# A two-layer image kernel: inverse roots on GpSimd, the LayerNorm variance with positions on partitions, and a new order within the scan's step

## The chip, the cores and the metric

The kernel runs on one core of a Trainium2 chip, as one launch. The metric is the device time of that launch in microseconds (us). Before the change the median of three runs is 4572.44 us (4570.81 to 4586.5). Five engines take part, each with its own queue of instructions: TensorE (PE in the profile, with its weight loads as PEld), VectorE (DVE), ScalarE (ACT), GpSimd (POOL) and SyncE (SP), which here only starts DMAs.

## The reference

The input is `x` of shape (4, 48, 48, 128). Two layers are computed, each as `x = x + layer(groupnorm(x))`. The change touches the first layer nearly alone:

```python
def _L0_conv_ref(x, ...):                       # d = 256, N = 16 states, K = 4 directions, R = 8
    xin, z = split(x @ in_proj_w.T)             # 256 + 256 channels
    xc = silu(depthwise_conv_3x3(xin) + conv_b)
    xs = stack([rows, columns, rows reversed, columns reversed])    # 4 directions of 2304 positions
    dts_r, Bs, Cs = split(x_proj(xs))
    dt = softplus(dt_proj(dts_r) + dt_proj_b)
    A  = -exp(A_logs)
    h  = h * exp(dt * A) + (dt * u) * B         # a scan over the positions, for 256 channels x 16 states
    y  = sum_n(h * C) + Ds * xs                 # the four directions are summed
    y  = (y - mean(y)) * rsqrt(var(y) + 1e-05) * norm_g + norm_b    # over the 256 channels
    return (y * silu(z)) @ out_proj_w.T

def _gn(v, G=32, eps=1e-5):                     # ahead of both layers
    return (v - mean) / sqrt(var + eps)         # mean and var over a group of 4 channels
```

The second layer (Fourier operators and an attention over 32 heads) gets only its group norm's root changed.

## The kernel before

**Layout.** In the first layer the channels lie on the partitions, as two halves `f` of 128, and the positions along the free axis. An image has 2304 positions in five chunks of 480, 480, 480, 480 and 384. The order of the work is image by image, four directions each in the order `ORDER` (0, 2, 1, 3), five chunks each (backwards for directions 2 and 3), and 16 states each: 4 x 4 x 5 x 16 = 1280 steps. The layer takes the span from about 60 to 3779 us; the second layer follows it.

**The step.** `advance` (L807) puts a new step into a window of nine and runs the list `LAGS` (L800-804): each stage works on the step that lies so many places back, so the work of one step is spread over nine turns of the loop. Every instruction of the first layer is recorded by one helper (class `Ordered`, all of them line L55 in the profile), which keeps each engine in program order. So the place of a stage in `LAGS` is its place in the queues. The stages are:

- `fetch` loads the row of C for the step into `cbc`, on SP's queue, spread over the partitions by the DMA. `cbc` has four buffers.
- An even state is "plain": PE transposes a column of B into `pb` (`spread`), DVE multiplies `db = du * pb` (`drive_in`), POOL writes the two columns between the halves from the carry (`open_db`), and ACT's Exp writes the decay into PSUM, tile `da` (`decay_here`).
- An odd state is "turned": ACT scales a transposed `du` by B (`scaled`, stage `scale`), PE transposes that back into PSUM `da` (`turn`), and ACT's Exp writes `decay` into SBUF (`decay_there`).
- `scan`: one DVE instruction, `h = decay * h + db` along the positions, for both halves. Its two forms in the profile are `h<-da,carry,db` (plain) and `h<-decay,carry,da` (turned).
- `carry_on` copies the last column of `h` for the next chunk, and `read_out` multiplies `hc = h * cbc`, both on POOL.
- `sum_plain` and `sum_turned`: PE transposes `hc` and adds it up over the states in PSUM `yp`. After state 15 `put_away` has ACT copy `yp` to the tile `turned`, and sends it to memory or starts `gather`.

**The side work.** All else is written as generators that stand in the list `later`: `end_piece` and `begin_piece` (two entries of `LAGS`) run one of them by one piece each step. `begin_piece` runs a generator up to its next PE work, and `end_piece` runs what follows on the other engines. The generators that matter here are: `front` (L249: group norm, `widen`, and ten `convolve`s of the next image), `project` and `project_chunk` (dt, B and C of a chunk for the next direction), `turn_du` (the transposed `du`), `gather` (the two directions of a chunk brought together), `back` (L460: LayerNorm, gate and output projection of one chunk, five for each image, 20 in all) and `matrices` (L263: during the last image it builds what the second layer needs, from many small DMAs on SP's queue). `front` or `matrices` starts when no `back` of the image before is left. After `begin()` all side work shares one PSUM bank, tag `pp`.

**ACT's tables.** ACT holds the tables of a set of functions; where the next function is not in the set, the program has an `ACT_TABLE_LOAD`. The step needs Exp, and the gates need Tanh, which stand with no load between them. `clump` (L445) runs Softplus over the dt of a whole direction. It is called at state 4 of the last chunk (L892-894), ahead of the step. `back` takes the inverse root of the variance as `exp(-0.5 * ln(v + eps))`: Ln at one yield and Exp in place two pieces later, both on 128 x n values, since `lnmat` (a 128 x 128 matrix of 1/256) puts the variance on every partition. `group_affine` (L911), called once for each image and twice in the second layer, takes Sqrt on ACT and a reciprocal on DVE.

**Idle transposes.** `warm` (L781) has PE transpose the identity three times into the bank `pp`, on every second step, if no side work is held on PE. Nothing reads the result.

The planner has no costs and no due times; the order of the queues is the order in which the generators and stages run.

Of the kernel before, what the change touches and what calls it, by code (L numbers as in the profile page):

```python
# [10 lines left out]
F32 = mybir.dt.float32  # L11
BF16 = mybir.dt.bfloat16
AF = mybir.ActivationFunctionType
ALU = mybir.AluOpType
# [44 lines left out]
def first_layer(ctx, tc, io, x1_dram, sp_dram, d_w, d_m):  # L59
# [79 lines left out]
        on.vector.tensor_scalar(w_out[:, 0, f], w_out[:, 0, f], ln_g[:, f : f + 1], None, ALU.mult)  # L139
    eps = const.tile([128, 1], F32, name="eps")  # L140
    on.gpsimd.memset(eps, 1e-5)
    ddiag = const.tile([128, NF, 128], F32, name="ddiag")
    for f in range(NF):
        on.vector.tensor_scalar(ddiag[:, f], ident, ds_sum[:, f : f + 1], None, ALU.mult)
# [26 lines left out]
    def open_up(b, x, made):  # L171

        xc = two.tile([128, NF, L], F32, tag="xc", name=f"xc{b}")
        made["xc"] = xc
        st = small.tile([128, 6, 6], F32, tag="st", name=f"st{b}", bufs=1)
        for q in range(6):
            on.vector.bn_stats(st[:, q], x[:, 0, q * 384 : (q + 1) * 384])
            if q % 2:
                yield FREE
        mv = small.tile([128, 2], F32, tag="mv", name=f"mv{b}")  # L180
        on.vector.bn_aggr(mv, st)
        aff = small.tile([128, 2], F32, tag="aff", name=f"aff{b}")
        group_affine(on, small, ps_s, gmat, eps, mv[:, 0:1], mv[:, 1:2], aff[:, 0:1], aff[:, 1:2], 1, f"g{b}")
        yield FREE
        wb = small.tile([128, NF], F32, tag="wb", name=f"wb{b}")
        pw = side(f"pw{b}")
        for f in range(NF):
            on.tensor.matmul(
                pw[:, f : f + 1], w_z[:, f * 128 : (f + 1) * 128], aff[:, 1:2], start=True, stop=True
            )  # L190
        on.scalar.activation(wb, pw[:, 0:NF], AF.Copy, scale=0.5)
        w = two.tile([128, D], F32, tag="w", name=f"w{b}")
        on.gpsimd.tensor_scalar(w, w_z, aff[:, 0:1], None, ALU.mult)
        made["w"], made["wb"], made["aff"] = w, wb, aff
        yield FREE

    def widen(b, x, aff, engine):

# [11 lines left out]
    def convolve(b, f, pad, xc, s, n):  # L210
        ends = (1, 3, 5, 7, 8) if b < 2 else (1, 2, 3, 4, 5, 6, 8)
        r0, nr = s // H, n // H
        pc = side(f"pc{b}_{f}_{s}")
        for j in range(9):
            dy, dx = divmod(j, 3)
            on.tensor.matmul(
                pc[:, 0:n].rearrange("p (r c) -> p r c", c=H),
                w_c[:, j, f * 128 : (f + 1) * 128],
                pad[:, r0 + dy : r0 + dy + nr, dx : dx + H],
                start=(j == 0),  # L220
                stop=(j == 8),
            )
            if j in ends:
                yield None if j == 8 else MORE
        v = xc[:, f, s : s + n]
        th = one.tile([128, LC], F32, tag="th", name=f"th{b}_{f}_{s}")[:, 0:n]
        on.scalar.activation(v, pc[:, 0:n], AF.Identity, bias=cb[:, f : f + 1], scale=0.5)
        on.scalar.activation(th, pc[:, 0:n], AF.Tanh, bias=cb[:, f : f + 1], scale=0.5)
        on.vector.scalar_tensor_tensor(v, th, 1.0, v, ALU.add, ALU.mult)

    def boot(chunks, made):

# [144 lines left out]
    def project_chunk(c, w_dt, xc):  # L377


        k, s, n = c.k, c.s, c.n  # L380
        if k < 2:
            src = at(xc, k, s, n)
            px = side(f"px{c.t}")
            for f in range(NF):
                on.tensor.matmul(
                    like(px[0 : PAIR + NX, 0:n], k), w_xp[:, k, f], src[:, f], start=(f == 0), stop=(f == NF - 1)
                )
                yield MORE if f == 0 else None
# [41 lines left out]
    def project(b, k, chunks, xc):  # L430
# [11 lines left out]
        projected.append(chunks)  # L442
        yield FREE

    def clump():  # L445

        while projected:
# [12 lines left out]
    def back(b, s, n, yb, x, w, wb):  # L460
# [9 lines left out]
        xp = one.tile([128, LC], F32, tag="th", name=f"xp{t}")[:, 0:n]  # L470
        on.gpsimd.tensor_copy(like(xp, 1), xs)
        pm = side(f"pm{t}")
        for f in range(NF):
# [4 lines left out]
        on.scalar.activation(z[:, :, 0:n], ys, AF.Square)  # L478
        yield FREE
        pv = side(f"pv{t}")  # L480
        for f in range(NF):
            on.tensor.matmul(pv[:, 0:n], lnmat, z[:, f, 0:n], start=(f == 0), stop=(f == NF - 1))
        yield

        on.scalar.activation(rs[:, 0:n], pv[:, 0:n], AF.Ln, bias=eps)
        yield FREE
        for f in range(NF):
            pz = side(f"pz{t}_{f}")
# [300 lines left out]
    step_i = [0]  # L789

    def drain(gen):
        if gen in later:
            later.remove(gen)
# [4 lines left out]

    decay_here, decay_there = partial(decay, turned=False), partial(decay, turned=True)
    LAGS = (  # L800
        (8, sum_plain), (3, fetch), (2, open_db), (4, drive_in), (5, scan), (3, spread), (7, sum_turned),
        (3, decay_there), (6, carry_on), (4, turn), (2, scale), (4, decay_here), (None, end_piece), (8, put_away),
        (None, begin_piece), (None, warm), (5, read_out),
    )
    window = deque([None] * 9, 9)

    def advance(u):  # L807
        window.appendleft(u)
        step_i[0] += 1
        for lag, stage in LAGS:  # L810
            if lag is None:
                stage()
# [42 lines left out]
    for j, chunks in enumerate(directions):  # L855
# [8 lines left out]
        for m, c in enumerate(chunks):  # L864
            c.carry = carries[j % 2]
            c.next = chunks[m + 1] if m + 1 < len(chunks) else directions[j + 1][0] if k < 2 else None
            for i in range(N):
# [66 lines left out]
def layer1(ctx, tc, io, x1_dram, out):  # L934
# [38 lines left out]
    fw = load("fw", [128, 66], io["c_FW"])  # L973
    eps = const.tile([128, 1], F32, name="eps1")
    nc.gpsimd.memset(eps, 1e-5)
    mean_m = const.tile([128, 32], F32, name="mean_m")
    nc.gpsimd.memset(mean_m, 1.0 / (H * W))
    over_h = const.tile([H, H], F32, name="over_h")
# [21 lines left out]
    def statistics(psum, p, x):  # L1000
# [8 lines left out]
        group_affine(on, small, psum, gmat, eps, mv[:, :, 0], mv[:, :, 1], aff[:, 0], aff[:, 1], 2, f"l1{p}")  # L1009
        return aff  # L1010

    def forward_w(psum, work, p, x, aff):
# [1173 lines left out]
```

## Time and profile before

| | us |
|---|---|
| median of three runs | 4572.44 |
| the profiled run | 4572.95 |
| its span | 4571.2 |
| around the span | 1.75 |
| first layer, boot (to about 60) | 60 |
| first layer, 1280 steps | about 60 to 3745 |
| last `back` and change of layers | 3745 to 3803 |
| second layer | 3803 to 4571 |

The page's table of the costliest groups gives the size of the parts. A line has: source line, engine, operation, the tile written and those read, the shapes, the count, then the busy time and the mean duration of one in ns, and the idle time just before them with what ended most of it. "(+1 forms)" says that chunks of 384 are averaged in.

```profile
L55 POOL TENSOR_TENSOR hc<-h,cbc 128x960 f32<-128x960 f32 (+1 forms) x1280 | 2544.1, 1990 | 618.7 <-PE yp L55 228.0
L55 DVE TENSOR_TENSOR_SCAN h<-da,carry,db 128x962 f32<-128x962 f32 (+1 forms) x640 | 1356.5, 2120 | 145.7 <-ACT da L55 136.8
L55 DVE TENSOR_TENSOR_SCAN h<-decay,carry,da 128x962 f32<-128x962 f32 (+1 forms) x640 | 1363.3, 2130 | 12.7 <-PE da L55 6.4
L55 DVE TENSOR_TENSOR db<-du,pb 128x960 f32<-128x960 f32 (+1 forms) x640 | 700.4, 1094 | 99.6 <-PE pb L55 88.0
```

DVE is thus busy for 3854.3 of 4571.2 us (84%), PE for 85%, ACT for 77%, POOL for 73%.

### The profile page before, as it was taken

To read this page: it belongs to the slowest core of one execution; us is meant where nothing else is said; L and a number is where in the kernel's file an instruction comes from. 1 tells how busy PE (TensorE), PEld (TensorE's weight loads), DVE (VectorE), ACT (ScalarE), POOL (GpSimd) and SP (SyncE) were. 2 spreads that over 40 slices of the span, in tenths; PEclk is the share of its full clock that TensorE was granted. 3 is DMA by queue.
4 is the path that set the end of the run, shared out by engine and by line. 5 is a ranking of instruction groups with operands and counts; after the bars stand their busy time and mean duration, and the time that the engine had idled before them with its cause. 6 is when DMAs were issued, how large, how long until landed. Compare 5 with 4: busy or idle time off the path is not lost. (4 is left out here: it accounts for less than half of the span.)

```text
span 4571.2 us, 74429 instructions
## 1 busy us (share of the span) xinstructions
PE 3878.1 (85%) x26572; PEld 3020.8 (66%) x26572; DVE 3854.3 (84%) x2646; ACT 3510.6 (77%) x7002; POOL 3335.4 (73%) x3494
## 2 busy tenths in 40 slices
PE   6989988888999878889998788878887875979877
PEld 3777777776777767767777677667777752545543
DVE  3988899989999999999989999979999974656446
ACT  3888888998888889988888899879999862323344
POOL 2777788878887888878878888768888861456432
PEclk8989999999999999999999999989999997989877
DMA  2334333333343343334333333334433332155536
GB/s 62 90 90 109 93 97 100 109 95 106 101 106 95 97 106 104 97 101 109 102 93 103 106 104 94 104 87 113 104 103 106 99 111 58 26 130 136 129 101 159
DMA packets 327070, 461.08 MB, mean 101 GB/s; under 512 B 112788, under 2 KB 295636, under 8 KB 325996
## 3 DMA queue, kind: packets, MB, share of 16 engines
q1 hardware_dynamic: 311904, 433.20, 36.0%
q10 hardware_dynamic: 14796, 23.13, 1.5%
q8 instruction: 210, 3.44, 0.3%
q14 instruction: 160, 1.31, 0.1%
HBM read 400.99 MB, written 55.44 MB: 100 GB/s over the span
## 5 line engine op out<-in xcount | busy, mean ns | idle before, releaser
L55 POOL TENSOR_TENSOR hc<-h,cbc 128x960 f32<-128x960 f32 (+1 forms) x1280 | 2544.1, 1990 | 618.7 <-PE yp L55 228.0
L55 DVE TENSOR_TENSOR_SCAN h<-da,carry,db 128x962 f32<-128x962 f32 (+1 forms) x640 | 1356.5, 2120 | 145.7 <-ACT da L55 136.8
L55 DVE TENSOR_TENSOR_SCAN h<-decay,carry,da 128x962 f32<-128x962 f32 (+1 forms) x640 | 1363.3, 2130 | 12.7 <-PE da L55 6.4
L55 PE MATMUL yp<-ident,hc 128*128 128x128 f32 (+1 forms) x9728 | 1221.5, 278 | 48.1 <-POOL hc L55 47.4
L55 PEld LDWEIGHTS yp<-ident,hc 128*128 128x128 f32 (+1 forms) x9728 | 1110.6, 141 | 198.0 <-issue 111.2
L55 ACT ACTIVATE scaled<-turned,bt 128x256 f32<-128x256 f32 (+1 forms) x2432 | 1034.4, 497 | 2.8 <-PE da L55 2.7
L55 ACT ACTIVATE da<-dt,a_neg 128x480 f32<-128x480 f32 (+1 forms) x1280 | 826.4, 646 | 191.2 <-DVE h L55 167.9
L55 ACT ACTIVATE decay<-dt,a_neg 128x480 f32<-128x480 f32 (+1 forms) x1280 | 800.1, 675 | 58.1 <-DVE h L55 34.0
L55 PE MATMUL da<-ident,scaled 128*128 128x128 f32 (+1 forms) x4864 | 640.1, 274 | 191.8 <-DVE h L55 174.2
L55 DVE TENSOR_TENSOR db<-du,pb 128x960 f32<-128x960 f32 (+1 forms) x640 | 700.4, 1094 | 99.6 <-PE pb L55 88.0
L55 PEld LDWEIGHTS da<-ident,scaled 128*128 128x128 f32 (+1 forms) x4864 | 537.3, 144 | 238.3 <-DVE h L55 103.3
L55 PEld LDWEIGHTS pb<-ident,bt 128*128 128x128 f32 (+1 forms) x2432 | 290.6, 140 | 178.5 <-issue 110.0
L55 PE MATMUL pb<-ident,bt 128*128 128x128 f32 (+1 forms) x2432 | 373.0, 275 | 34.9 <-DVE db L55 34.3
L55 PE MATMUL pc<-pad,w_c 128*128 128x480 f32 (+1 forms) x720 | 335.1, 579 | 13.3 <-ACT th L55 8.0
L55 POOL TENSOR_TENSOR du<-dt,xc 128x480 f32<-128x480 f32 (+1 forms) x160 | 205.9, 1287 | 49.3 <-ACT dt L55 49.3
L1599 POOL TENSOR_TENSOR v<-grep,xrep 128x768 f32<-128x768 f32 x96 | 174.9, 1823 | 90.5 <-PE acc L1603 48.8
L1603 PE MATMUL acc<-v,attn_c 128*64 128x384 f32 x1152 | 211.7, 505 | 28.9 <-DVE v L1595 15.7
L1595 DVE TENSOR_TENSOR v<-gp,xrep 128x1536 f32<-128x1536 f32 x96 | 167.9, 1756 | 77.5 <-PE acc L1603 44.7
L55 PEld LDWEIGHTS da<-carry,ident 128*128 128x128 f32 x1280 | 200.0, 197 | 0.0
L55 PE MATMUL da<-carry,ident 128*128 128x2 f32 x1280 | 196.7, 223 | 0.0
L55 POOL COPY carry<-h 128x2 f32<-128x2 f32 x1024 | 195.7, 191 | 0.0
L1603 PEld LDWEIGHTS acc<-v,attn_c 128*64 128x64 f32 x1152 | 120.2, 140 | 109.2 <-issue 51.9
(378 smaller groups left out, 4208.0 us busy)
## 6 DMA issues: line engine op xcount, KB each, us to landing
cbc<-cd SPq DMA_DIRECT2D x512, 240.0 KB
cbc<-other SPq DMA_DIRECT2D x512, 240.0 KB
xrep<-dxt SPq DMA_DIRECT2D x48, 576.0 KB
cbc<-cd SPq DMA_DIRECT2D x128, 192.0 KB
cbc<-other SPq DMA_DIRECT2D x128, 192.0 KB
yt<-turned ACTq DMA_DIRECT2D x40, 384.0 KB
old<-yt SPq DMA_DIRECT2D x40, 384.0 KB
grep<-dgt SPq DMA_DIRECT2D x16, 576.0 KB
```

Source lines behind the costliest of these rows:

```text
L55: return lambda *args, **kw: self._tc.keep_in_program_order(emit(*args, **kw))
L1595: nc.vector.tensor_mul(v, gp[:, None, :, 0:NC].to_broadcast([128, 2, 2, NC]), x[:, :, 0:2])
L1599: nc.gpsimd.tensor_mul(v3, r[:, 2:3].to_broadcast([128, 2, NC]), x[:, :, 2])
L1603: nc.tensor.matmul(acc[c][64 * b : 64 * b + 64, 0:NC], attn_c[:, 2 * pair + b, g, q], v[:, b, c] if c < 2 else v3[:, b], start=first, stop ...
```

## The change

The change has seven parts, all in the order of the diff:

- `back`: the variance is taken with the positions on the partitions, by one-column matmuls (`pv`, one column for each block of 128 positions), copied to `var` with eps added on ACT (Identity), raised to -0.5 on POOL (`ALU.pow` on 128 x 4), transposed back onto all partitions by PE (`pe`) and copied to `rs` by ACT. Ln and Exp go. There is one more pair of yields.
- `group_affine`: DVE adds 1e-5, POOL raises to -0.5, for Sqrt and reciprocal. It applies in both layers.
- `convolve`: the gate's last product is held back; `flush`, a new entry of `LAGS`, issues it in the next step, ahead of the scan. `project_chunk` flushes all first.
- `soften`: the softplus at state 4 of the last chunk is issued by an entry of `LAGS` within the step.
- `warm` is gone.
- `LAGS` has a new order; `fetch` goes from lag 3 to 2, `drive_in` from 4 to 3, and `put_away` from 8 to 7.
- In the first direction a further piece of side work runs in every third step, for every fifth.

```diff
+    half = const.tile([128, 1], F32, name="half")
+    on.gpsimd.memset(half, -0.5)
+    var = const.tile([LB, 4], F32, name="var")
+    on.gpsimd.memset(var, 1.0)
...
+    held_back = deque()
+
+    def later_on(work):
+        held_back.append([1, work])
+
+    def flush(every=False):
+        for item in list(held_back):
+            item[0] -= 1
+            if every or item[0] <= 0:
+                held_back.remove(item)
+                item[1]()
...
         on.scalar.activation(th, pc[:, 0:n], AF.Tanh, bias=cb[:, f : f + 1], scale=0.5)
-        on.vector.scalar_tensor_tensor(v, th, 1.0, v, ALU.add, ALU.mult)
+        later_on(lambda: on.vector.scalar_tensor_tensor(v, th, 1.0, v, ALU.add, ALU.mult))
...
         if k < 2:
+            flush(True)
             src = at(xc, k, s, n)
...
+    def soften():
+        if wanted[0]:
+            wanted[0] = False
+            clump()
...
         pv = side(f"pv{t}")
-        for f in range(NF):
-            on.tensor.matmul(pv[:, 0:n], lnmat, z[:, f, 0:n], start=(f == 0), stop=(f == NF - 1))
+        for q, r in blocks(n):
+            for f in range(NF):
+                on.tensor.matmul(
+                    pv[0:r, q : q + 1],
+                    z[:, f, q * LB : q * LB + r],
+                    lnmat[:, 0:1],
+                    start=(f == 0),
+                    stop=(f == NF - 1),
+                )
         yield
-        on.scalar.activation(rs[:, 0:n], pv[:, 0:n], AF.Ln, bias=eps)
+        for q, m, r in runs(n):
+            on.scalar.activation(var[0:r, q : q + m], pv[0:r, q : q + m], AF.Identity, bias=eps[0:r])
+        on.gpsimd.tensor_tensor(var, var, half.to_broadcast([LB, 4]), ALU.pow)
+        yield FREE
+        pe = side(f"pe{t}")
+        for q, r in blocks(n):
+            on.tensor.transpose(
+                pe[:, q * LB : q * LB + r], var[0:r, q : q + 1].to_broadcast([r, 128]), ident[0:r, 0:r]
+            )
+        yield
+        on.scalar.copy(rs[:, 0:n], pe[:, 0:n])
         yield FREE
...
-            if f == 0:
-                on.scalar.activation(rs[:, 0:n], rs[:, 0:n], AF.Exp, scale=-0.5)
...
-    def warm():
-        n = (384, 0)[step_i[0] % 2]
-        if n and current[0] is None:
-            p = ps_s.tile([128, 512], F32, tag="pp", name=f"warm{step_i[0]}")
-            for q in range(0, n, 128):
-                on.tensor.transpose(p[:, q : q + 128], ident, ident)
...
     LAGS = (
-        (8, sum_plain), (3, fetch), (2, open_db), (4, drive_in), (5, scan), (3, spread), (7, sum_turned),
-        (3, decay_there), (6, carry_on), (4, turn), (2, scale), (4, decay_here), (None, end_piece), (8, put_away),
-        (None, begin_piece), (None, warm), (5, read_out),
+        (8, sum_plain), (2, fetch), (None, flush), (5, scan), (3, spread), (None, soften), (7, sum_turned),
+        (2, scale), (4, turn), (3, decay_there), (4, decay_here), (2, open_db), (None, end_piece),
+        (None, begin_piece), (6, carry_on), (3, drive_in), (5, read_out), (7, put_away),
     )
...
                 if nxt is not None and (4, 4) == (m, i):
                     drain(nxt)
-                    clump()
+                    wanted[0] = True
                 advance(Step(c, i))
-                if not j and not chunks[-1].ready and i % 5 == 0:
+                if not j and not chunks[-1].ready and i % 3 == 0:
                     piece()
...
-def group_affine(nc, pool, psum, gmat, eps, mean, var, scale, shift, n, name):
+def group_affine(nc, pool, psum, gmat, half, mean, var, scale, shift, n, name):
...
-    nc.scalar.activation(sd, pv[:, 0:n], AF.Sqrt, bias=eps)
-    nc.vector.reciprocal(scale, sd)
+    nc.vector.tensor_scalar(sd, pv[:, 0:n], 1e-5, None, ALU.add)
+    nc.gpsimd.tensor_tensor(scale, sd, half.to_broadcast([128, n]), ALU.pow)
```

The tiles `th` and `xp` share one buffer, before and after (`bufs=1` is now written out).

More of the change, by code (lines that the diff above doesn't have):

```diff
@@ L182, in open_up @@
         aff = small.tile([128, 2], F32, tag="aff", name=f"aff{b}")
-        group_affine(on, small, ps_s, gmat, eps, mv[:, 0:1], mv[:, 1:2], aff[:, 0:1], aff[:, 1:2], 1, f"g{b}")
+        group_affine(on, small, ps_s, gmat, half, mv[:, 0:1], mv[:, 1:2], aff[:, 0:1], aff[:, 1:2], 1, f"g{b}")
         yield FREE
@@ L225, in convolve @@
         v = xc[:, f, s : s + n]
-        th = one.tile([128, LC], F32, tag="th", name=f"th{b}_{f}_{s}")[:, 0:n]
+        th = one.tile([128, LC], F32, tag="th", bufs=1, name=f"th{b}_{f}_{s}")[:, 0:n]
         on.scalar.activation(v, pc[:, 0:n], AF.Identity, bias=cb[:, f : f + 1], scale=0.5)
         on.scalar.activation(th, pc[:, 0:n], AF.Tanh, bias=cb[:, f : f + 1], scale=0.5)
-        on.vector.scalar_tensor_tensor(v, th, 1.0, v, ALU.add, ALU.mult)
+        later_on(lambda: on.vector.scalar_tensor_tensor(v, th, 1.0, v, ALU.add, ALU.mult))
     def boot(chunks, made):
@@ L443, in project @@
         yield FREE
+    wanted = [False]
+    def soften():
+        if wanted[0]:
+            wanted[0] = False
+            clump()
     def clump():
@@ L469, in back @@
         rs, xo = ws[:, NF * LC : (NF + 1) * LC], ws[:, (NF + 1) * LC : (NF + 2) * LC]
-        xp = one.tile([128, LC], F32, tag="th", name=f"xp{t}")[:, 0:n]
+        xp = one.tile([128, LC], F32, tag="th", bufs=1, name=f"xp{t}")[:, 0:n]
         on.gpsimd.tensor_copy(like(xp, 1), xs)
@@ L779, in piece @@
         begin_piece()
-    def warm():
-        n = (384, 0)[step_i[0] % 2]
-        if n and current[0] is None:
-            p = ps_s.tile([128, 512], F32, tag="pp", name=f"warm{step_i[0]}")
-            for q in range(0, n, 128):
-                on.tensor.transpose(p[:, q : q + 128], ident, ident)
-    step_i = [0]
     def drain(gen):
@@ L808, in advance @@
         window.appendleft(u)
-        step_i[0] += 1
         for lag, stage in LAGS:
@@ L975, in layer1 @@
     nc.gpsimd.memset(eps, 1e-5)
+    half = const.tile([128, 1], F32, name="half1")
+    nc.gpsimd.memset(half, -0.5)
     mean_m = const.tile([128, 32], F32, name="mean_m")
@@ L1008, in statistics @@
         aff = small.tile([128, 2, 2], F32, tag=f"aff{p}", name=f"aff{p}", bufs=1)
-        group_affine(on, small, psum, gmat, eps, mv[:, :, 0], mv[:, :, 1], aff[:, 0], aff[:, 1], 2, f"l1{p}")
+        group_affine(on, small, psum, gmat, half, mv[:, :, 0], mv[:, :, 1], aff[:, 0], aff[:, 1], 2, f"l1{p}")
         return aff
```

## The prediction

> **What bounds the kernel now.** I read first the busy time by windows. From 1010 to 1915 us, all of one image, DVE is busy 849.55 of 905 us, PE 794.21, ACT 795.93, POOL 754.24. DVE is thus the bound of the steps, with 55 us of idle time in an image. Two steps without a stall take two scans and one `db` product: by the timeline 2.13 + 2.115 + 1.05 = 5.285 us, eight pairs 42.28 us, and several chunks (image 1, direction 1) take just that. No part of the change takes work off DVE in the steps. So I ask only for DVE's waits. The second view is the waits of DVE alone, from 115 to 3745 us (what it waited for: us in total, times, longest).
>
> ```profile
> DVE h L55 <- ACT da L55: 127.1, 73, 8.0
> DVE db L55 <- PE pb L55: 67.8, 83, 3.7
> DVE xc L55 <- ACT th L55: 12.2, 14, 1.4
> DVE ws L55 <- ACT ws L55: 10.8, 10, 3.1
> DVE db L55 <- POOL db L55: 9.5, 5, 3.3
> DVE h L55 <- POOL carry L55: 8.2, 2, 6.0
> DVE h L55 <- POOL hc L55: 6.9, 3, 4.5
> DVE aff L55 <- ACT gs_g L55: 2.9, 3, 1.0
> ```
>
> The whole list sums to 257 us, and half of it is the plain scan that waits for ACT's decay. ACT is 88% busy in an image, so a few us of extra work reach DVE. The third view, the groups of ACT, has that work:
>
> ```profile
> L55 ACT ACT_TABLE_LOAD x95 | 121.9, 1283 | 58.4 <-PE gv_l L55 34.7 <-DMA a_neg<-in_A_logs 12.6 <-PE gv_g L55 9.8
> ```
>
> The fourth view is the timeline of ACT (start, duration, operation) in one `back`, and the scan of DVE that follows:
>
> ```profile
> 1042.92 1.28 ACT L55 ACT_TABLE_LOAD   x1
> 1044.22 0.66 ACT L55 ACTIVATE ws<-pv,eps 128x480 f32<-128x480 f32 x1
> 1044.78 1.70 ACT L55 ACTIVATE scaled<-turned,bt 128x256 f32<-128x256 f32 x4
> 1046.48 1.28 ACT L55 ACT_TABLE_LOAD   x1
> 1047.77 0.60 ACT L55 ACTIVATE ws<-ws 128x480 f32<-128x480 f32 x1
> 1050.54 1.36 ACT L55 ACTIVATE da<-dt,a_neg 128x480 f32<-128x480 f32 x2
> ```
>
> ```profile
> 1051.99 2.22 DVE L55 TENSOR_TENSOR_SCAN h<-da,carry,db 128x962 f32<-128x962 f32 x1 [2.01 <-ACT da L55]
> ```
>
> Two loads, Ln and Exp, 3.8 us of ACT, delay `da`, and DVE stands for 2.01 us.
>
> **The change, part by part.** The sum is made against the profiled run, 4572.95 us (its span 4571.2 and 1.75 around it), which is 0.5 us above the median of the runs.
>
> *Loads of the 20 backs.* Out: 2 x 1.283 + 0.645 + 0.58 = 3.79 us of ACT each. In: one or two Identity copies of `var` (nearest row `wb<-pw` 128x2, 0.17 us) and the copy of `pe` (`yb<-pg` 128x480, 0.56 us), about 0.9. Net -2.9 us of ACT per back. The stalls of DVE that follow such a pair in the timeline are 1.70, 0.43, 1.91, 2.01, 1.07 in image 0, the like in images 1 and 2, and 1.70, 2.02, 2.02, 3.10 in image 3: 29.3 us in all. Each is shorter than 2.9, so nearly all go; the last waits for other work too. I take **-27** (-29 to -15, if ACT is late again at the copy). [...]
>
> The new path has waits of its own. `pe` stands in PE's queue behind the POOL power, which stands behind the `hc` product of the step before (1.99 us). Behind `pe` stand PE's `yp`, `pb` and `da`, and DVE waits for these. PE is 88% busy in an image, so it has 0.3 us of slack in a step of 2.64. The trace has no power. Its nearest row is POOL's TENSOR_TENSOR on 96x32 values, 0.242 us; the upper bound is `hc`, 1.99 us. PE waits between 0 (POOL ahead) and 2 us per back; I take 0.2 of DVE time for each of 20, **+4** (0 to +34, at 2.0 less 0.3). The eight one-column matmuls (two records each, as `da<-carry`, 0.223) and four transposes (0.275), for four records of 0.566, are +2.4 us of PE a back, in two pieces, and take the place of the idle transposes. The extra pair of yields moves the rest of a back, and the `front` after it, by some four steps; `front` is drained only two directions later: 0.
>
> *Group norm.* In the boot and in layer 1 the table load lies on the chain: 2.32 and 2.34 us of DVE idle. A DVE add (0.16) and a power (0.24) with three handovers of some 0.07 (the boot's rows have 0.03 to 0.08) come to 0.6 for 1.83 us from the end of `gv` to `aff`: -1.2 each. Sqrt's return load made a scan wait 1.74 us at 313.5. Against that, in images 1 to 3 DVE waits at `aff` 0.97 us each for ACT and will wait for POOL, with an `hc` of up to 1.99 ahead: about nil. Together **-4** (-9 to +4).
>
> *Gate's product.* `xc <- th` is 12.2 us above. The product now stands behind the next step's `sum_plain` and ahead of its scan, yet in most cases between the same DVE instructions as before; two in ten in images 2 and 3 move behind a `db` product of 1.05 us. Half of the wait, **-6** (-12 to 0). The boot's own waits stay, as each projection flushes first.
>
> *Order: `fetch`.* Image 3's `matrices` floods SP's queue. From 2950 to 3075 us POOL waits for `cbc`:
>
> ```profile
> POOL hc L55 <- DMA cbc<-cd: 29.7, 10, 7.5
> ```
>
> and DVE behind it 24.3 us (the three POOL rows of DVE's waits in that window, 9.5 + 8.2 + 6.6). With lag 2 each load stands one step, 2.64 us, earlier, ahead of that step's small DMAs. Of the longest wait of 7.5 us this is a third: **-9** (-24 to 0). With four buffers the load for step u needs the one of step u-4, which `read_out` uses in turn u+1; the load stands in turn u+2, before in u+3. If SP is ahead it waits there, and the `old`, `xd` and x1 transfers behind it wait too; they are needed some turns later, so 0 for that.
>
> *Order: `put_away`.* ACT's copies of `yp` come one step earlier, right behind the last sum on PE, and ahead of the next `scaled`. From the end of PE's last `yp` and ACT's position there, most of 70 chunks have ACT idle or PE done; I estimate **+3** (0 to +10). *`drive_in`, `open_db`, the rest*: the new lag and the new place cancel, and the queues of DVE, PE and POOL have the steps' instructions in the same order as before, so **0** (0 to +5, if POOL is held by a power). *Softplus in the step*: ACT's order is the same, **0**; its 15 stalls of up to 8.04 us (66.6 us in all) stay.
>
> *First direction.* 67 to 337 us has DVE at 220.90 of 270.00. Chunks 1 to 4 have 23.6 us of idle time; more pieces bring `project` earlier. **-5** (-20 to +5, as the same ACT work comes in denser).
>
> *No idle transposes.* 660 records of 0.273 us, about 0.53 us for a triple, leave PE's queue. PE is not the bound, so that alone is worth little: `db <- pb`, 67.8 us, is the row to gain on. But the granted clock speaks against it. Busy time by windows (length, then PE, PEld, DVE, ACT, POOL, clock, DMA share, GB/s):
>
> ```profile
> 1580.90:1584.30 3.40, 1.81 (x18) 1.83 (x18) 3.40 (x2) 2.78 (x8) 3.40 (x5) 1.00 0.62 164
> 1584.30:1587.70 3.40, 2.13 (x18) 1.66 (x17) 3.40 (x4) 3.37 (x8) 3.18 (x5) 1.00 0.58 160
> 2567.34:2570.76 3.42, 0.56 (x4) 0.35 (x4) 3.42 (x4) 3.39 (x8) 1.84 (x3) 1.00 0.01 2
> 2570.76:2574.17 3.41, 3.41 (x17) 3.41 (x18) 3.41 (x3) 2.76 (x7) 3.38 (x3) 0.50 0.63 213
> ```
>
> Clock changes fall on a grid of 3.413 us. A window with PE busy 0.56 of 3.42 is followed by one at half clock; 1.81 of 3.40 (53%) is not. Of the 42 drops to half clock in the steps, 39 follow a share of 51% or less. At 1580.9 us `warm` holds 0.53 of the 1.81: without it 47%. Twelve windows fall from above 50% to below so. [...] The DVE waits on `pb` after a drop are 0.4 to 1.7 us; 12 x 0.7 = **+8** (-5, if the shorter PE queue helps `pb`, to +20).
>
> *Tail.* From 3745 to 3779 the last back runs alone as one chain; `var`, the power, `pe` and its copy for two loads, Ln and Exp: **+2** (-2 to +4).
>
> Sum: -27 + 4 - 4 - 6 - 9 + 3 - 5 + 8 + 2 = -34; 4572.95 - 34 = **4539 us**, 0.7% less.
>
> **The rivals.** *Hidden gain.* The ACT time won in a back is lost again at the next stall: DVE's stalls on `da` and `pb` alternate, and a DVE that isn't held by ACT meets PE sooner. For it: 83 waits on `pb`. Against it: the chunks of 42.28 us show that PE can keep up with an unstalled DVE. If half of the gains (51) go, -25 + 17 = -8: **4565 us**, within 0.5%.
>
> *Slower by the clock.* Without `warm` PE sits near the edge. At half clock PE does 1.7 us of work in a window of 3.41 that brings 3.0 (88%), and DVE waits for up to the 1.3 us of difference. 53 full-clock windows in the steps have a share below 56% once `warm` is out of them. If all drop: 53 x 1.3 = +69 in place of +8, so -34 + 61 = +27: **4600 us**. The kernel is slower from 33 such windows on (-42 + 33 x 1.3), by over 0.5% from 50. Against it: some windows at 42 to 50% do not drop today, and at 2574 us, after a half-clock window, DVE did not wait at all.
>
> *A dear power.* At 1.99 us for each of 20 the queue of POOL holds `carry`, `db` and `hc`; POOL is 83% busy in an image, with 0.45 us to spare in a step: 20 x (2.0 - 0.45) = +31 in place of +4: **4566 us**. Above any row of POOL, from 3.5 us on (20 x 3.05 = +61), it makes the kernel slower by 0.5%.
>
> **How the numbers follow.** Forecast 0.55, hidden gain or a power of 2 us 0.22, clock 0.13, dearer power or a queue that I did not see 0.10. Taken as independent, the distances of the terms' ends add as squares: 27 down and 39 up, 4512 to 4578, the forecast's own range. Towards the clock case it reaches 4600, and as far below for gains that are larger together (all loads, `fetch` and the first direction by half their ends): **4495 to 4600**. A difference under 0.5% (23 us) is what a measurement here can't tell from none. Faster by more (below 4550): 0.58; within: 0.22; slower (above 4595): 0.20.
>
> **What would show it.** Right: 49 loads on ACT; `da` in DVE's waits near 95 us; the stalls on `ws <- ws` gone; POOL rows of DVE's waits lower around 3000 us. Wrong: a row `pe <- var` or `pb` among PE's waits of over 10 us behind POOL's power; a power above 2 us; more than 20 further half-clock windows with longer `db <- pb`; an `h <- carry` or `hc` row that grows outside image 3.

## The result, and the profile after

The changed kernel takes a median of 4536.76 us (4521.50 to 4538.54, six runs) beside 4570.76 us (4563.92 to 4586.50, six runs) of the kernel before: a ratio of 0.9913 with a 95% interval of 0.9891 to 0.9935. Run once more (below) it had 0.9897 (0.9873 to 0.9920). So it is 0.9 to 1.0% faster, some 40 to 47 us; 34 us, to 4539 us, were forecast. Two slow runs are left out of all comparisons, one of the kernel before (7237.86 us, granted clock 0.922) and one of the old list with idle transposes (9075.08 us, 0.48).

The profiled execution has a span of 4534.9 us, 36.3 less than before. The page's busy times and the groups of the two scans and the `db` product, in the columns of before:

```profile
PE 3854.2 (85%) x26212; PEld 2993.0 (66%) x26212; DVE 3854.3 (85%) x2646; ACT 3439.2 (76%) x6964; POOL 3356.7 (74%) x3523
L55 DVE TENSOR_TENSOR_SCAN h<-da,carry,db 128x962 f32<-128x962 f32 (+1 forms) x640 | 1355.9, 2119 | 115.7 <-ACT da L55 97.3
L55 DVE TENSOR_TENSOR_SCAN h<-decay,carry,da 128x962 f32<-128x962 f32 (+1 forms) x640 | 1362.5, 2129 | 6.5 <-PE da L55 6.2
L55 DVE TENSOR_TENSOR db<-du,pb 128x960 f32<-128x960 f32 (+1 forms) x640 | 699.0, 1092 | 110.1 <-PE pb L55 100.1
```

DVE is busy for 3854.3 us, to the tenth what it was (3854.3). All of the gain is idle time of DVE, as it has to be if DVE bounds the steps. ACT lost 71.4 us of busy time, 48 table loads (97 to 49) and the Ln and Exp, less what was added. In the trace of before 45 of the loads stand right ahead of an Exp, 20 of an Ln, 20 of a Softplus and 8 of a Sqrt, and 39 of the 40 Tanh of the `convolve`s have none beside them. DVE's waits over the steps, the view of the prediction, now read (115 to 3710 us, as the last scan ends at 3709 us; us in total, times, longest):

```profile
DVE h L55 <- ACT da L55: 97.3, 48, 7.5
DVE db L55 <- PE pb L55: 78.4, 84, 3.9
DVE ws L55 <- PE pr L55: 8.3, 3, 2.8
DVE db L55 <- POOL db L55: 6.6, 3, 4.4
...
DVE xc L55 <- ACT th L55: 5.0, 8, 1.0
DVE ws L55 <- PE po L55: 3.9, 4, 1.1
DVE h L55 <- POOL hc L55: 3.6, 2, 3.4
DVE h L55 <- POOL carry L55: 2.2, 2, 2.0
DVE aff L55 <- POOL aff L55: 2.0, 3, 0.7
...
DVE ws L55 <- ACT ws L55: 1.2, 5, 0.4
```

Row against row: the scan's wait for ACT fell by 29.8 us and `ws <- ACT ws` by 9.6, the three POOL rows by 12.2 (24.6 to 12.4), the gate's wait by 7.2. On the other side `db <- PE pb` grew by 10.6, and `ws` waits for PE (`pr` and `po`) by 10.4. These rows sum to -37.8, the whole lists to -34.2 (256.9 us before, 222.7 now), beside 36.3 measured. The rows that grew by over 2 us are all waits for PE, and the experiments turn on them.

The loads, the power and its neighbours on ACT, from the groups (busy us, mean ns):

```profile
L55 ACT ACT_TABLE_LOAD x47 | 60.3, 1283 | 13.6 <-DMA a_neg<-in_A_logs 12.5 <-ACT a L55 0.3
```

```profile
L55 POOL TENSOR_TENSOR var<-var,half 128x4 f32<-128x4 f32 x20 | 20.4, 1020 | 11.4 <-ACT var L55 11.4
L55 POOL TENSOR_TENSOR aff<-gs_g,half 128x1 f32<-128x1 f32 x4 | 2.3, 563 | 33.1 <-DVE gs_g L55 33.1
```

A power of 128x4 takes 1.02 us, one of 128x1 0.56 us, four times and twice the nearest row that the trace of before had, and half of the upper bound. The timeline of ACT in the back that was shown before:

```profile
1035.88 0.39 ACT L55 ACTIVATE var<-pv,eps 128x3 f32<-128x3 f32 x2
1036.17 1.70 ACT L55 ACTIVATE scaled<-turned,bt 128x256 f32<-128x256 f32 x4
1039.27 0.56 ACT L55 COPY ws<-pe 128x480 f32<-128x480 f32 x1 [1.40 <-PE pe L55]
1039.72 1.28 ACT L55 ACTIVATE decay<-dt,a_neg 128x480 f32<-128x480 f32 x2
```

Where two loads, Ln and Exp stood there are 0.95 us of work, and ACT waits 1.40 us for `pe`. The weight load of `pe` begins at 1038.13 us, as the power has just ended (1038.08 us) and PE has just come to the end of the loads of `yp`, at half clock (granted clock 0.50 from 1035.62 to 1039.03 us). DVE shows no idle time from 1028 to 1042 us: the wait lies in slack.

The gain has a place. By the starts of DVE's scans, direction by direction (us, after less before):

| direction | image 0 | image 1 | image 2 | image 3 |
|---|---|---|---|---|
| 0 | +2.4 | +5.1 | +7.4 | -14.8 |
| 2 | -4.8 | +0.6 | +0.7 | +0.8 |
| 1 | -1.0 | +2.1 | +5.3 | -0.3 |
| 3 | -8.5 | -10.1 | -11.7 | -7.4 |

Three of the five backs of an image take their root in its direction 3 (the powers at 846, 932 and 983 us in image 0), and all four images gain there. Direction 0 of images 1 and 2 holds the other two backs of the image before and the `front`, and gives 5 to 7 us back (that this is because the `front` now comes later was not tested); in image 3 `matrices` stands there and 14.8 us are gained. Direction 1 of images 1 and 2 loses 2 and 5 us, with no back in it: of the change it has the list of stages, the place of one gate's product, and the idle transposes that are gone. The last one was not in the prediction.

### The profile page after: what moved, and what is told of

Its sections match the earlier page's. It is cut to its first block, busy times and chain, and to the rows that moved or that the text cites. A ratio compares the mean times of both kernels' runs of the same rounds, so it can differ in the third digit from the quotient of the medians.

```text
span 4534.9 us, 73722 instructions
## 1 busy us (share of the span) xinstructions
PE 3854.2 (85%) x26212; PEld 2993.0 (66%) x26212; DVE 3854.3 (85%) x2646; ACT 3439.2 (76%) x6964; POOL 3356.7 (74%) x3523
## 4 chain that ended last, share of the span: by engine, by line
PE 35%; ACT 22%; DVE 21%; issue 12%; POOL 5%; DMA 3%; SPq 1%; ACTq 0%; DVEq 0%; POOLq 0%
DVE h L55 13%; PE yp L55 8%; ACT scaled L55 6%; PE pc L55 5%; DVE db L55 4%; ACT da L55 4%; PE da L55 4%; ACT decay L55 4%; PE pd L55 2%; POOL hc L55 2%; PE acc L1634 2%; ACT dt L55 2%; ACT turned L55 2%; PE pg L55 2%; PE pb L55 2%
## 5 line engine op out<-in xcount | busy, mean ns | idle before, releaser
L55 PE MATMUL yp<-ident,hc 128*128 128x128 f32 (+1 forms) x9728 | 1268.6, 283 | 52.9 <-POOL hc L55 49.3
L55 PEld LDWEIGHTS yp<-ident,hc 128*128 128x128 f32 (+1 forms) x9728 | 1140.6, 145 | 217.5 <-issue 109.3
```

The costliest lines, as they stand in the source:

```text
L55: return lambda *args, **kw: self._tc.keep_in_program_order(emit(*args, **kw))
```

## The experiments

Each kernel ran with five rounds beside the kernel before. In the first four one part is taken alone or undone.

**The power alone.** On the kernel before: `back` and `group_affine` as in the change, all else as before.

```diff
-        on.scalar.activation(rs[:, 0:n], pv[:, 0:n], AF.Ln, bias=eps)
...
+        on.gpsimd.tensor_tensor(var, var, half.to_broadcast([LB, 4]), ALU.pow)
```

> The kernel before with the root by the power alone (back and both group norms); the idle transposes, the order of the step and the gate's product as before. My theory, by the terms of the prediction: -27 (loads of the backs) +4 (PE behind the power) -4 (group norm) +2 (tail) = -25 us, DVE's wait 'h <- ACT da' at about 95 in place of 127, 49 table loads. Rival 'hidden gain': half of it or less, -12 us, with 'db <- PE pb' larger by the rest. Rival 'the new order did it': within 5 us of the kernel before.

4552.99 us, ratio 0.9948 (0.9930 to 0.9966), which is -24 us (-16 to -32). DVE's wait for `da` is 101.6 us in its profile. The term of the prediction for this part was -25. The rivals "half of it" and "the new order did it" fall for the mean, though in the profile `db <- PE pb` grew too:

```profile
DVE h L55 <- ACT da L55: 101.6, 45, 8.0
DVE db L55 <- PE pb L55: 86.8, 79, 5.2
...
DVE ws L55 <- PE pr L55: 8.3, 3, 2.8
```

The 8.3 us of `pr` are here as well, so they belong to this part; the likely reason, not tested, is that the last pieces of the longer `back` come later.

**No idle transposes, alone, and put back.**

```diff
-        (None, begin_piece), (None, warm), (5, read_out),
+        (None, begin_piece), (5, read_out),
```

> The kernel before without the idle transposes, all else as before. My theory: +8 us (some 12 more drops to half clock in the steps, 0.7 us each). Rival 'clock': a drop costs some 5 us, so +20 us and more, with 'db <- PE pb' larger by that. Rival 'PE's queue': the triples only delayed PE, so -5 us, and fewer waits on pb.

Alone on the kernel before: 4580.94 us, ratio 1.0020 (1.0002 to 1.0039), +9 us (+1 to +18): the theory, with the two rivals outside the interval. By the recorded clock changes, from the first scan to the end of the last, its profile has 53 drops to half clock and 300 us there, for 42 drops and 236 us before.

```diff
+        (None, begin_piece), (None, warm), (6, carry_on), (3, drive_in), (5, read_out), (7, put_away),
```

> The changed kernel with the idle transposes put back, at the place that they had after begin_piece. My theory: -8 us against the changed kernel (about 4529). Rival 'clock': -20 us (about 4517), with the time at half clock in the steps back from 313 to about 235 us. Rival 'PE's queue': no gain, or slower by 5 us, since the idle transposes now stand ahead of work that PE has to do.

Put back into the changed kernel: 4534.73 us, ratio 0.9904 (0.9886 to 0.9922). That is no faster than without them (0.9913 and, run again, 0.9897), though in the profiles there are 38 drops and 242 us at half clock for 48 and 294 without them. (The 313 us in the expectation end at 3745 us and so count 20 us that lie behind the last scan.) A second profile of the changed kernel has 44 drops and 256 us, so single profiles leave the number open by some. The +9 us on one kernel and nothing on the other are both measured; the two intervals are wide enough for a common price of a few us.

**The old list of stages.** The changed kernel with the lags and places of before, `flush` ahead of `scan` and `soften` ahead of the decays.

```diff
-        (8, sum_plain), (2, fetch), (None, flush), (5, scan), (3, spread), (None, soften), (7, sum_turned),
+        (8, sum_plain), (3, fetch), (2, open_db), (4, drive_in), (None, flush), (5, scan), (3, spread), (7, sum_turned),
...
```

> The changed kernel with the old list of stages (fetch at lag 3, drive_in at 4, put_away at 8; flush ahead of the scan and softplus ahead of the decays kept, no idle transposes). My theory: the order is worth -9 (fetch) +3 (put_away) = -6, so this kernel is 6 us slower than the changed one, about 4543, and the difference lies in image 3's chunks 1 to 4 of the first direction. Rival 'order is nothing': within 3 us. Rival 'put_away hurts': 5 us or more faster than the changed kernel.

4528.76 us, ratio 0.9892 (0.9875 to 0.9909). The intervals of the two lists overlap, and the changed kernel run again (next) has 4529.34 us: the order as a whole is nothing that the totals of these runs can measure.

**Gate, first direction and order, each alone on the kernel before, and the changed kernel once more.**

```diff
-        on.vector.scalar_tensor_tensor(v, th, 1.0, v, ALU.add, ALU.mult)
+        later_on(lambda: on.vector.scalar_tensor_tensor(v, th, 1.0, v, ALU.add, ALU.mult))
```

> The kernel before with the gate's product held back to the next step (flush ahead of the scan, and in project_chunk), all else as before. My theory: -6 us, with DVE's wait 'xc <- ACT th' at 5 to 6 in place of 12.2 from 115 us on. Rival 'kept neighbours': the product stays between the same DVE instructions in eight of ten places, so within 3 us. Rival 'missing gain': the parts measured so far (power -24, no transposes +9) leave some -20 us of the change's -36 to the other parts; if it is here, -12 us or more.

```diff
-                if not j and not chunks[-1].ready and i % 5 == 0:
+                if not j and not chunks[-1].ready and i % 3 == 0:
```

> The kernel before with a further piece in every third step of the first direction, for every fifth; all else as before. My theory: -5 us, all of it before 340 us. Rival 'denser ACT': 0 to +5 us, since in the changed kernel the first direction is 2.4 us longer than before. Rival 'missing gain': -12 us.

```diff
-        (8, sum_plain), (3, fetch), (2, open_db), (4, drive_in), (5, scan), (3, spread), (7, sum_turned),
+        (8, sum_plain), (2, fetch), (5, scan), (3, spread), (7, sum_turned), (2, scale), (4, turn), ...
```

> The kernel before with the new list of stages (fetch 2, drive_in 3, put_away 7, the new places; idle transposes kept behind begin_piece; gate's product and softplus as before). My theory: -6 us, -9 of it in image 3 from 2818 to 3077 us. Rival 'order costs': the old list on the changed kernel gave a median 8 us lower, so +8 us here, with 'db <- PE pb' larger. Rival 'order is nothing': within 3 us.

> The changed kernel once more, to stand beside the old list of stages and the idle transposes by more runs. My theory: a median within 5 us of 4537, and runs spread over some 15 us as before, because the half-clock windows fall at other places from run to run. Rival: a median near 4529, and then neither the order nor the idle transposes made a difference to it.

| kernel | median us | ratio | interval |
|---|---|---|---|
| gate alone | 4584.49 | 1.0015 | 0.9998 to 1.0032 |
| first direction alone | 4578.72 | 0.9998 | 0.9977 to 1.0018 |
| new order alone | 4571.10 | 0.9991 | 0.9969 to 1.0012 |
| changed, again | 4529.34 | 0.9897 | 0.9873 to 0.9920 |

None of the three can be told from nothing by itself. In the profile of the gate alone its row `xc <- ACT th` falls from 12.2 to 2.7 us, and `db <- PE pb` rises from 67.8 to 90.0. With -24 for the power and +9 for the transposes the parts, each by its ratio of the kernel before, sum to some -13 us, where the whole has 40 to 47. Either two parts make something together, or something else moves in all of these runs.

**The power with one further part.**

```diff
+        later_on(lambda: on.vector.scalar_tensor_tensor(v, th, 1.0, v, ALU.add, ALU.mult))
```

> The kernel before with the power and the gate's product held back; order, first direction and idle transposes as before. By single runs: power -21, gate +4, so -17 if they add. My theory now: the change's gain beyond the power (some -24 of -46) comes from the power's shorter ACT work together with another part, since each other part alone gave nothing; with the gate -35 us. Rival 'first direction': -17 to -21 here, and -35 with the denser pieces. Rival 'chance of the clock': the one profile of the power alone held 22 us of half-clock stalls in images 1 and 2 and its mean was pulled up by such; then -25 to -30 in both.

4539.28 us, ratio 0.9912 (0.9888 to 0.9936): -40 us (-51 to -29), nearly the whole change.

```diff
+                if not j and not chunks[-1].ready and i % 3 == 0:
```

> The kernel before with the power and a further piece in every third step of the first direction; gate, order and idle transposes as before. Single runs add to -23. My theory (gate with power): -23. Rival 'first direction': -35, of it -8 before 580 us against the power alone, as the four kernels with both have it. Rival 'chance of the clock': -25 to -30.

4569.42 us, ratio 0.9981 (0.9965 to 0.9996): -9 us (-16 to -2), less than the power alone. By "theory gate with power" the first is a hit and the second should have been -23; the rival "chance of the clock" wanted 25 to 30 in both, the rival "first direction" 35 in the second. All have misses.

**Old list with idle transposes.** The changed kernel with both restored.

```diff
+        (None, begin_piece), (None, warm), (5, read_out),
```

> The changed kernel with the old list of stages and the idle transposes (power, group norm, gate, softplus in the step and denser pieces kept). If the idle transposes are worth 9 us as on the kernel before, 9 us below the old list without them: some -55 us against the kernel before, 4520. Rival 'worth nothing here': -46, as the changed kernel with them put back was no faster than without. Less half-clock time in the steps than 328 us either way.

Ratio 0.9903 (0.9879 to 0.9927), -44 us, for 0.9892 without them: on the changed kernel the transposes are worth nothing that can be seen with the old list either. What was expected of the time at half clock was not measured.

Set side by side, the totals say which parts matter. The seven measured versions that have both the power and the held-back gate lie between 0.9890 and 0.9913 (the one of the last experiment below among them); the six that lack one or both lie between 0.9948 and 1.0020. But the gate's product is not shown to earn its 16 us where it stands. Of the 23.9 us between the profiles of the power alone and of the power with the gate, 16.1 lie in direction 1 of images 1 and 2, which holds one gate each.

**What moves.** The traces record changes of TensorE's clock, between 1.0 and 0.5. In each trace read here the times of all changes after 60 us are the same modulo 3.413 us (3.41333 us fits the traces of before and after best), within 5 ns of their median: the changes lie on a grid that runs through the whole execution. It lies differently against the start of each execution: its first edge falls 0.52 us after the start of the span in the profile of before, 1.38 us in that of after. In direction 1 of images 1 and 2, where the work is the same in every kernel but for the list of stages, the idle transposes and the place of one gate's product, I read where on this grid the second chunk's first scan starts and how long the chunk takes:

| kernel | image 1: us after an edge, chunk us | image 2 |
|---|---|---|
| changed | 0.20, 47.67 | 0.08, 47.67 |
| changed, again | 0.15, 47.68 | 0.99, 42.28 |
| transposes put back | 1.08, 42.29 | 0.27, 48.06 |
| power alone | 0.26, 46.46 | 0.50, 44.70 |
| gate alone | 0.21, 46.67 | 0.72, 42.28 |
| power with gate | 0.51, 44.70 | 1.17, 42.29 |
| first direction alone | 0.86, 42.28 | 0.03, 46.44 |
| new order alone | 0.50, 44.80 | 1.17, 42.28 |
| old list | 0.90, 42.29 | 0.82, 42.28 |
| power, first direction | 0.97, 42.28 | 0.98, 42.29 |
| no transposes alone | 0.94, 42.29 | 1.54, 42.28 |
| before | 1.60, 42.28 | 1.54, 42.29 |

From 0.72 to 1.60 us after an edge the chunk runs without a stall; from 0.03 to 0.51 it loses 2.4 to 5.8 us, whatever the kernel. Other places did not occur in these executions. The second row is one kernel in one execution, with the same instructions in both images.

The first chunk of the same direction shows that the place is not all. With the old list of stages the seven chunks that start 0.00 to 0.31 us after an edge take 51.9 to 54.8 us; with the new list the three that start at 0.14 to 0.30 take 45.2, as at the other places. So in this chunk the order of the stages does matter, at some places on the grid. The third to fifth chunks take the same time in all of these kernels, to 0.05 us, wherever they start. The windows of the changed kernel show what happens (length, PE, PEld, DVE, ACT, POOL, granted clock, DMA share, GB/s):

```profile
1516.70:1520.10 3.40, 1.90 (x15) 1.67 (x16) 3.40 (x2) 3.40 (x9) 2.54 (x4) 1.00 0.35 111
1520.31:1533.96 13.65, 13.65 (x57) 11.58 (x56) 9.74 (x7) 7.07 (x17) 9.27 (x12) 0.50 0.29 80
```

PE has 1.90 us of work in one window of the grid (56% of it), the granted clock is 0.50 for the next four, and DVE loses 3.91 of 13.65 us. The timeline of DVE names the waits:

```profile
1523.92 2.19 DVE L55 TENSOR_TENSOR_SCAN h<-da,carry,db 128x962 f32<-128x962 f32 x1
1529.23 1.16 DVE L55 TENSOR_TENSOR db<-du,pb 128x960 f32<-128x960 f32 x1 [3.12 <-PE pb L55]
1531.17 2.22 DVE L55 TENSOR_TENSOR_SCAN h<-decay,carry,da 128x962 f32<-128x962 f32 x1 [0.79 <-PE da L55]
...
1539.86 2.22 DVE L55 TENSOR_TENSOR_SCAN h<-da,carry,db 128x962 f32<-128x962 f32 x1 [1.18 <-ACT da L55]
```

3.12 + 0.79 + 1.18 are 5.1 of the 5.4 us that this chunk has over 42.28. In the prediction a drop cost 0.7 us.

**The test of it: added work that should make the kernel faster.**

```diff
+                if k == 1 and 0 < b < B - 1 and (m, i) == (0, 6):
+                    for _ in range(4):
+                        on.vector.tensor_mul(idle, idle, idle)
                 advance(Step(c, i))
```

> The changed kernel with four idle products of 128x64 on VectorE (together some 0.8 us) ahead of step 6 of the first chunk of direction 1, in images 1 and 2; nothing else. In the profiles so far the second chunk of that direction takes 42.3 us when its first scan starts 0.57 to 1.65 us after an edge of the 3.413 us grid of clock changes, and 44.7 to 48.1 us when it starts 0.08 to 0.51 us after one; the changed kernel starts it at 0.20 and 0.08. Theory 'grid': the delay moves the start to about 1.0 and 0.9, the chunk takes 42.3 us in both images, and in the profile direction 1 of both gets 4 to 5 us shorter, though work is added. Rival 'work': direction 1 gets 0.8 us longer in each image, and chunk 1 stays at 47.7. The time over all runs is some 5 to 9 us below the changed kernel by the first (4521 to 4526), 2 us above it by the second.

The bounds that this expectation gives for the start differ from the table by up to 0.15 us; the table stands.

The windows of the second chunk of image 2, in the changed kernel and in this one:

```profile
2428.33:2476.00 47.67, 41.70 (x279) 36.77 (x277) 42.59 (x25) 37.31 (x79) 38.47 (x42) 0.82 0.33 96
```

```profile
2421.37:2463.65 42.28, 34.72 (x269) 30.35 (x267) 42.28 (x25) 37.36 (x79) 38.39 (x42) 0.96 0.43 108
```

The chunk takes 42.29 us in image 1 and 42.28 in image 2, at 1.67 and 0.90 us after an edge (1.0 and 0.9 expected). In image 2 one window at half clock is left in it (granted clock 0.96), which cost nothing. The first chunk got 0.71 us longer in each, so direction 1 is 4.69 and 4.65 us shorter than in the changed kernel. Only image 2 is a test of the delay. There direction 1 began 2.72 us after an edge, for 2.63 in the changed kernel, so without the 0.71 us the second chunk would have begun at 0.19, where every chunk stalled. In image 1 direction 1 began at 0.10, for 2.75, ahead of any delay; without it the chunk would have begun at 0.96, where none did. So "grid" is shown for this place, by image 2 and by the order of the table, and "work" is out. Over all runs the kernel has 4524.34 us, 0.9890 (0.9873 to 0.9907), inside the 4521 to 4526 expected; its interval overlaps that of the changed kernel, so that the whole is faster is not shown.

No version with the power and the held-back gate can be told from the best of them, this one: their intervals all overlap.

## Why the prediction was right, point by point

*Loads of the backs, -27: right.* The two rows that wait for ACT lost 39.4 us, and the later end of a `back` put 10.4 into waits on `pr` and `po`: -29. Alone, with the group norms, -24 (-16 to -32).

*PE behind the power, +4: right in number, wrong in cause.* The power takes 1.02 us, not 0.242, and `pe` waits for it on PE in 15 of the 20 backs, 17.4 us in all; the prediction had named over 10 us there as a sign of being wrong. Yet DVE pays nothing for it that can be seen. Its idle intervals over 0.25 us in the 8 us after each of the 20 powers sum to 3.8 us, and all of that lies in three backs, behind a drop of the clock (the last section has the windows). The likely cover is the slack of PE and the depth of the step.

*Group norm, -4: about right.* The first scan starts at 66.63 us for 67.77 (-1.1, with -1.2 worked out). In images 1 to 3 DVE now waits 2.0 us for the power and 1.6 for `gv`, for 2.9 before (`aff <- ACT gs_g`). In layer 1 the wait at `aff` was 2.34; it is 0.68 for `gv` and 0.82 for the power, with an add of 0.16 between.

*Gate, -6: the row was right, the effect alone not seen.* `xc <- th` fell from 12.2 to 5.0. Alone the time went by +7 us (-1 to +15); on the power by a further -16, with intervals that just overlap, and most of that in the profiles lies where hardly a gate stands.

*`fetch`, -9: not shown.* In direction 0 of image 3 the three rows of DVE's waits on POOL are 24.3 us before, 12.2 after, 13.6 with the old list on the changed kernel and 16.8 with the new order alone, so most of the fall comes with the other parts too. With the old list on the changed kernel that direction took 4.8 us longer, which speaks for it; with the new order alone it took 3.3 us longer than before, which speaks against. So the part of the order stays open.

*`put_away`, the rest of the order, +3: within what can be measured*, as the whole order is worth -4 us (-14 to +5) alone. It was not tried piece by piece.

*First direction, -5: not seen.* -1 us (-11 to +8) alone; the first two directions together gained 2.4 us in the changed kernel.

*No idle transposes, +8: right on the kernel before (+9), nothing on the changed one.* On the kernel before the drops rose by 11 (42 to 53), where 12 were forecast. Between the changed kernel with the transposes and without them they rose too, from 38 to 48 (44 in the second profile), and nothing was lost. So the step that does not carry over is the 0.7 us for a drop: in the changed kernel the drop at 1520.31 us cost DVE 5.1 us, and those at 1544.20 and 1561.27 us, in the same chunk, nothing. The reading of 51% as the edge was too sharp as well: the window at 1516.9 us had 56% and was followed by a drop. And 7 of the 48 drops of the changed kernel follow windows that hold the matmuls of another part of the change, the new variance, which the prediction had down as 2.4 us of PE a back in place of the transposes (the last section).

*Tail, +2.* The last back ends 40.3 us after the start of the last scan, for 36.7: +3.6.

*The rivals.* "Slower by the clock" had the mechanism, PE at half clock and DVE waiting on `pb`, and a price per drop that was met in places; but where it had 53 windows drop, 6 drops were added. A power of 2 us did not come. The "hidden gain" was met in part: `db <- PE pb` grew by 10.6 us, where it had 25 of the gains go. The lower end of the range, 4495 us, does not come out of the terms that are named for it; nothing hung on it.

The forecast of -34 for 36 in the profile owes something to luck. Its largest term, the loads, has the right mechanism and size. But `fetch`, gate and first direction, -20 together, could not be shown one by one, the +4 and the +8 were met by other causes or not at all in the changed kernel, and a term of some 10 us, where the grid falls (2 x 5.4 us in the second chunks alone), was not in it.

## What to carry to other kernels

Count table loads (1.28 us each here), and where ACT is 88% busy, look for the wait that follows each pair; a root by a power on an engine with room (1.02 us here) takes them out, and its own latency was hidden here. Where runs of one kernel spread by 0.3 to 0.5% and single parts don't add up, compare the chunks of the traces one by one before a part is given the credit: here equal work took 42.3 or 47.7 us by its place on the clock's grid. With six to twelve runs the intervals here were some 0.2% to each side, so an edit worth 9 us or less needs more rounds on such a kernel, or a count of the stalls themselves. When matmuls are made very narrow, look at the granted clock behind them: here 50 of 200 busy windows with matmuls of one column were followed by a drop.

## What the runs showed of the hardware

The changes of TensorE's clock lay on a grid of 3.413 us, which did not move in 4.5 ms by more than 5 ns. One such window with PE 56% busy by the profile was followed by four at half clock. PE was busy in all of the four (13.65 of 13.65 us), and DVE waited 3.12 and 0.79 us for PE in them. The stretches at half clock in the steps of the same trace lasted one to five windows.

Windows with a high busy share of PE were followed by a drop too. In the new `back` the variance is made by matmuls of one column, up to 16 records of 0.25 us that overlap to 1.8 us a back, where four of 480 columns stood. A window of the changed kernel with 14 of them (1.36 of its 2.80 us of PE), the next one, and DVE's wait behind it:

```profile
929.80:933.21 3.41, 2.80 (x28) 2.71 (x27) 3.41 (x4) 3.26 (x9) 3.30 (x5) 1.00 0.42 149
933.21:936.62 3.41, 3.28 (x16) 3.26 (x17) 3.41 (x3) 2.94 (x7) 2.90 (x6) 0.50 0.34 81
```

```profile
938.55 1.16 DVE L55 TENSOR_TENSOR db<-du,pb 128x960 f32<-128x960 f32 x1 [1.04 <-PE pb L55]
```

PE is 82% busy, and the clock drops. In the steps of the eight profiles of kernels with the new root, 200 windows of the grid at full clock are at least 70% busy and hold such matmuls; 50 of them are followed by a drop. Of 6344 such windows without them, 10 are, and none of 823 in the kernel before. Less the time of these matmuls, the windows that dropped have shares of 24 to 52%. That is a drop behind 25% of the windows with matmuls of one column and behind 0.16% of those without; why was not shown, and no run tried another width. In the changed kernel they stand ahead of 7 of its 48 drops, and the three of these that DVE felt cost the 3.8 us named above.

The kernel fell into step with the grid, likely by its stalls. The two executions of the changed kernel began their first scan 0.40 and 0.83 us after an edge; from the second direction to the eighth their starts differ by at most 0.05 us on the grid (2.57 and 2.58, 0.22 and 0.21, 1.47 and 1.47, 0.40 and 0.38, 3.08 and 3.03, 2.75 and 2.71, 3.08 and 3.04). In the last experiment, whose kernel is the same up to image 1 but for one memset, the first scan began at 1.25 us and the next three directions within 0.08 us of the changed kernel's places, but the fifth 0.83 us off. So a small edit early in this kernel can move, for long stretches, the places on the grid, and with them the drops that are met later. That would explain why the parts of this change don't add. That the parts met different drops is seen in the traces; that this is all of the missing 30 us was only argued.

Four products of 128x64 on DVE, put in as a delay, took 3.19 us together where 0.8 were expected (single ones from 0.22 to 1.39 us), and cost 0.71 us, as the waits of 2.07 us that the first chunk of image 1 had (0.68, 0.34 and 1.05) are gone behind them. Why they were slow was not looked into.
